# Two bottleneck blocks on one core: the 3x3 convolution with four products over the columns in every row combination, and its differences on VectorE

## The chip, the cores and the metric

The kernel runs on one core of one Trainium2 chip. Its time is the device time of one execution in microseconds (us): 1990.88 us, the median of 4 runs (1990.1 to 1991.1). One further execution was recorded by the hardware profiler; all durations below come from that one. TensorE is called PE in the profile, VectorE DVE, ScalarE ACT, GpSimd POOL and SyncE SP.

## The reference

Two residual blocks of the ResNet kind, one after the other, all in fp32, on 64 images of 1024 channels and 14x14 pixels:

```python
def block(x, w1, b1, g1, be1, w2, b2, g2, be2, w3, b3, g3, be3, residual_scale):
    out = relu(bn(conv1x1(x, w1, b1), g1, be1))          # 1024 -> 256 channels
    out = relu(bn(conv3x3(out, w2, b2, pad=1), g2, be2)) # 256 -> 256
    out = bn(conv1x1(out, w3, b3), g3, be3)              # 256 -> 1024
    return relu(x + softplus(residual_scale) * out)
```

`bn` normalises by the mean and variance over all images and pixels of that same batch, so each convolution has to be complete before the next may use its result.

## The kernel before

The inputs of a block are laid out with the channels on the 128 partitions. The intermediate result with 256 channels stays on the chip (`y_all`: 128 partitions, 2 channel slots, all pixels). The program has these stages: the first 1x1 convolution of block 0 (from the start to about 308 us), the 3x3 convolution of block 0 (`conv2`, about 309 to 601 us), statistics, then the last 1x1 convolution of block 0 fused with the first of block 1 (to about 1290 us), the 3x3 convolution of block 1 (about 1294 to 1587 us), statistics, and the last 1x1 convolution with the way out. Beside the first stage `filters` makes the transformed 3x3 filters on VectorE and ScalarE and stores them in HBM through GpSimd's DMA queue, in 11 steps (`FSTEPS`) for each of 8 pieces.

**How the 3x3 convolution is computed.** It is a fast algorithm in both directions. The images are in 8 groups of 8 (`NG`, `GI`). Along the rows, four output rows are made from six *row combinations* of input rows (`NF` = 6, numbered 0 to 5): sums and differences with small factors. Each combination is multiplied with its own transformed filter, and the six products are combined into four output rows. Per group they come in the order 1, 2, 3, 4, 5, 0, so that there are 48 items in all. A combination has 2 slots of 32 lines (24 for combinations 3 and 4) of 14 columns per partition, which is 896 (672) numbers per partition. The columns are stored as the 7 odd ones and then the 7 even ones.

**Over the columns**, `FOUR` says which combinations use the cheaper form: all but combination 1. There the product has four parts instead of five, each with 4 matrix products over 7 columns (2 input slots x 2 output slots; each matrix product appears as two MATMUL records, so 8 records):
- `m`, on the sum of the odd and the even half (`sums`, line 596, VectorE). ScalarE copies it into the two output banks `even` and `odd` (line 699).
- `l`, on the difference of the halves (`diffs`, line 599, GpSimd). ScalarE copies it to a tile `ls` (line 699, called from `later`).
- `even` and `odd`, added into those banks, on `v` (line 603, VectorE): differences of neighbouring columns; ScalarE fills the two border columns (lines 607 and 608).

VectorE then adds or subtracts `ls` when it takes the result out of the banks (`add`, line 752).

Combination 1 has no `diffs`, no `v` and no `l`: `even` and `odd` read the combination itself with two filters each, which is 16 records for each of the two instead of 8, and its result is taken straight from the banks into the two tiles `a` and `d` (lines 785 and 786, four instructions). Its `m` copy adds the convolution's bias (line 697).

**The order of the work.** `combine` makes the row combinations of a pair on VectorE (line 581 is the helper `stt`, for scalar_tensor_tensor; lines 641, 643 and 648 are further instructions) and `ready` makes `sums`, `diffs` and `v` and issues the loads of the filters. The loop at the end of `conv2` holds a queue of three items that are ready. For item k it issues, in this order: `middle` (`l`), the `even` part, `start` of item k+1 (`m` and the two copies), a long piece of work on ScalarE (`long_work`: the normalisation of the next group or a moment of the last), the `odd` part, and then `finished.send`, which takes the item out and combines results (`finish`, lines 766 to 839). After that it makes item k+3. A scheduler that runs when the program is built merges the streams of instructions; the matrix products and the lines with `keep_in_program_order` keep their order. Each engine then works its list strictly in order.

For the last of the four output rows' parts (item 0 of a group), `finish` writes `out_rows[0]` from the banks (line 833) and adds `a` by an accumulating DMA from GpSimd (line 838), except in the last group, where VectorE adds it (line 831). The moments of group g-1 that long_work takes on ScalarE during group g need these rows.

The buffers are counted in `BUFS`. At the very end, `residual` for the last images writes the output in four transfers of two channel slots each, issued by SP (line 1086).

Of the kernel before, what the change touches and what calls it, by code (L numbers as in the profile page):

```python
# [41 lines left out]
P = 128  # L42
# [3 lines left out]
CS = C // P  # L46
# [23 lines left out]
BUFS = dict(ua=3, ub=3, t=2, r=4, sums=3, diffs=4, v=3, ls=3, f=2, fa=2)  # L70
# [3 lines left out]
FOUR = 0, 2, 3, 4, 5  # L74
NKS = [4 if i in FOUR else 5 for i in range(NF)]
NK = max(NKS)

FSTEPS = 11
D1D2, D0, D3, D1, D2 = range(5)
# [12 lines left out]
def bottlenecks(ctx: ExitStack, tc: tile.TileContext, x, w1s, w2s, w3s, pars, out):  # L92
# [10 lines left out]
        [dram.tile([P, MS, MS, NKS[i], P], FP, tag=f"u{b}_{i}", name=f"u{b}_{i}") for i in range(NF)]  # L103
# [70 lines left out]
    def filters(pieces, spare):  # L174
# [11 lines left out]
        c1 = view(second, 18, 5)  # L186
# [18 lines left out]
        for piece, following in itertools.zip_longest(pieces, pieces[1:]):  # L205
# [6 lines left out]
            def out(i, u, a=0):  # L212
                nc.gpsimd.dma_start(out=us[b][i][:, s, o, a : a + u.shape[1]], in_=u)
# [18 lines left out]
            yield  # L232
            sums(c2, c2, r1, ALU.subtract)
            scaled(r2, 1.0 / 2)
# [9 lines left out]
            yield  # L244

            sums(g[:, 0], g[:, 0], g[:, 2], ALU.add)
            scaled(c4, 1.0 / 48)
            out(4, c4)
            yield
            sums(c1[:, :3], g[:, 0], g[:, 1], ALU.add)  # L250
            yield
            sums(c1[:, 3:], c1[:, 0:3:2], c1[:, 1:2].to_broadcast([P, 2, P]), ALU.subtract)
            scaled(c1, -1.0 / 6)
            for to, a, e in ((D0, 0, 1), (D1D2, 1, 2), (D3, 2, 5)):
                out(1, c1[:, a:e], to)
# [293 lines left out]
    def conv2(psum, pool, b, par, aff, affine_of, stats):  # L549
# [32 lines left out]

        def combine(g, pair, before=None):
# [4 lines left out]
            def ready(i, r):  # L588
                lines = (full if i in (3, 4) else RT) * GI
                r = r.rearrange("p s r (i w) -> p s (r i) w", i=GI)  # L590

                def half(tag):
                    return pool.tile([P, MS, RT * GI, WH], FP, tag=tag, name=tag, bufs=BUFS[tag])[:, :, :lines]

                sums, diffs = half("sums"), None
                nc.vector.tensor_add(sums, r[:, :, :, WH:], r[:, :, :, :WH])  # L596
                if i in FOUR:
                    diffs = half("diffs")
                    nc.gpsimd.tensor_sub(diffs, r[:, :, :, :WH], r[:, :, :, WH:])  # L599
                    v = pool.tile([P, MS * RT * GI * W], FP, tag="v", name="v", bufs=BUFS["v"])  # L600
                    v = v[:, : MS * lines * W].rearrange("p (s l c) -> p s l c", s=MS, c=W)
                    q = r.rearrange("p s l (q c) -> p (s l) q c", q=2)
                    nc.vector.tensor_sub(
                        v[:, :, :, 1 : W - 1].rearrange("p s l (q c) -> p (s l) q c", q=2),
                        q[:, :, :, 1:], q[:, :, :, : WH - 1],
                    )
                    nc.scalar.activation(v[:, :, :, 0], r[:, :, :, 0], AF.Copy)
                    nc.scalar.activation(v[:, :, :, W - 1], r[:, :, :, W - 1], AF.Copy, scale=-1.0)
                    r = v

                first = g == 0 and i == order[0][0]
                u = {}
                for tag, a, e in (("ub", 1, NKS[i]), ("ua", 0, 1)) if first else (("ua", 0, 1), ("ub", 1, NKS[i])):
                    n = MS * MS * (NK - 1 if a else 1) * P
                    v = pool.tile([P, n], FP, tag=tag, name=tag, bufs=BUFS[tag])
                    v = v[:, : MS * MS * (e - a) * P].rearrange("p (s o k m) -> p s o k m", s=MS, o=MS, m=P)
                    for part in [slice(1, 2), slice(0, 1)] if first else [slice(0, MS)]:
                        nc.sync.dma_start(
                            out=v[:, part].rearrange("p s o k m -> p (s o) (k m)"),
                            in_=us[b][i][:, part, :, a:e].rearrange("p s o k m -> p (s o) (k m)"),  # L620
                        )
                    u[a] = v
                return Products(i, lines, r, sums, diffs, u, first)

            def run(ins):
                if before is not None:
                    tc.keep_in_program_order(ins)

            both = slice(0, MS)
            if pair[0] == 1:  # L630
                t1, t2 = new("t"), new("t")
# [10 lines left out]
                yield ready(1, ra)  # L642
                nc.vector.tensor_sub(rb, t1, t2)  # L643
                yield ready(2, rb)
            elif pair[0] == 3:
                t3, t4 = (new("t", full) for i in range(2))
# [8 lines left out]
            else:  # L655
                last(ra, g, 2, -4.0)
                last(rb, g, 1, -1.0)
                for s in range(MS):
                    stt(rb[:, s, :full], rows(g, s, 3, 0, full), -5.0, rows(g, s, 5, 0, full))
                    stt(ra[:, s, :full], rows(g, s, 2, 0, full), -5.0, rows(g, s, 4, 0, full))  # L660
                for s in range(MS):
                    stt(rb[:, s, :full], rows(g, s, 1, 0, full), 4.0, rb[:, s, :full])
                yield ready(NF - 1, rb)
                for s in range(MS):
                    stt(ra[:, s, 1:], rows(g, s, 0, 1, RT), 4.0, ra[:, s, 1:])
                yield ready(0, ra)

        class Products:


            def __init__(self, i, lines, r, sums, diffs, u, first):
                self.i, self.lines, self.n = i, lines, lines * WH
                self.r, self.sums, self.diffs, self.u, self.first = r, sums, diffs, u, first
                self.four = i in FOUR
# [17 lines left out]
            def biased(self, to, m):  # L692

                for v in to:
                    if self.i == 1:
                        for o in range(MS):
                            nc.scalar.activation(v[:, o], m[:, o], AF.Identity, bias=par[:, B2 + o : B2 + o + 1])
                    else:
                        nc.scalar.activation(v, m, AF.Copy)  # L699

            def later(self, k, v, op):

                l = self.whole("l", k, v)
                ls = pool.tile([P, MS * RT * GI * WH], FP, tag="ls", name="ls", bufs=BUFS["ls"])
                self.ls, self.op = ls[:, : MS * self.n].rearrange("p (o n) -> p o n", o=MS), op
                self.biased([self.ls], l)

            def start(self):
# [3 lines left out]
                if not self.first:  # L712
                    self.biased(self.banks.values(), self.whole("m", 0, self.sums))

            def middle(self):
                if self.four:
                    self.later(DIFF, self.diffs, ALU.subtract)

            def columns(self, *qs):

                r = self.r
                if self.four:
                    parts = {ODD: [(0, WH, D3M1, r[:, :, :, WH:])], EVEN: [(0, WH, D0M2, r[:, :, :, :WH])]}
                else:
                    parts = {
                        ODD: [(0, WH, D1, r[:, :, :, WH:]), (0, WH - 1, D3, r[:, :, :, WH + 1 :])],
                        EVEN: [(0, WH, D2, r[:, :, :, :WH]), (1, WH, D0, r[:, :, :, : WH - 1])],
                    }
                steps = [(q, o, part, s) for q in qs for o in range(MS) for part in parts[q] for s in range(MS)]
                if self.first:  # L730


                    steps.sort(key=lambda step: -step[3])
                opened = set()
                for q, o, (a, e, k, v), s in steps:
                    to = self.banks[q][:, o].rearrange("p (l c) -> p l c", c=WH)[:, :, a:e]
                    matmul(
                        to, self.filter(s, o, k), v[:, s], start=self.first and q not in opened, stop=True,
                        skip_group_check=True,
                    )  # L740
                    opened.add(q)
                if self.first:
                    self.later(0, self.sums, ALU.add)
# [6 lines left out]
            def add(self, q, to, v):  # L750

                nc.vector.tensor_tensor(to, v, self.column(q, self.ls), ALU.add if q == EVEN else self.op)  # L752
# [11 lines left out]
        def finish():  # L764


            for g in range(NG):
                out_rows = [y_grp[:, :, g, k::4, :] for k in range(4)]
                last_group = g == NG - 1

                def stat(k, lines):
# [5 lines left out]
                fa = None if ca.ls is None else outputs(ca)  # L777
                fb = outputs((yield))
                a, d = new("fa"), new("fb")
                if fa is not None:  # L780
                    nc.vector.tensor_add(a, fa, fb)
                    nc.vector.tensor_sub(d, fa, fb)
                else:
                    for q in ca.banks:
                        nc.vector.tensor_tensor(half(a, q), ca.column(q), half(fb, q), ALU.add)
                        nc.vector.tensor_tensor(half(d, q), ca.column(q), half(fb, q), ALU.subtract)
# [31 lines left out]
                if last_group:  # L818
# [3 lines left out]
                for j, q in enumerate(cb.banks):  # L822
                    for o in range(MS):
# [6 lines left out]
                        if last_group:  # L830
                            nc.vector.tensor_add(to, bank, more)
                        else:
                            nc.vector.tensor_tensor(to, bank, ls, ALU.add if q == EVEN else cb.op)
                    stat(2 + j, [out_rows[0][:, o].rearrange("p r (i q c) -> p q r i c", i=GI, q=2)[:, q] for o in range(MS)])
                if not last_group:
# [54 lines left out]
        def long_work(g, k):  # L890
# [4 lines left out]
            if g + 1 == NG:  # L895
                i = (None, 0, 1, 2, 3, None)[k]
# [13 lines left out]
        for k in range(NG * NF):  # L910
            item, more = queue[0], queue[1:2]
            item.middle()
# [4 lines left out]
            elif more and more[0].four:  # L917
# [156 lines left out]
    def residual(psum, xt, b, t, w3, aff, made=()):  # L1074
# [3 lines left out]
        step = 2 if b == 1 and t == T - 1 else CS  # L1078
        for o in range(CS):
# [3 lines left out]
            nc.scalar.activation(v, v, AF.Relu, bias=shift[:, o : o + 1])  # L1083
            if (o + 1) % step == 0:
                queue = nc.gpsimd if step == CS else nc.sync
# [298 lines left out]
```

## Time and profile before

| | |
|---|---|
| median of 4 runs | 1990.88 us |
| the profiled execution, its own time | 1990.68 us |
| its span (first to last instruction) | 1988.9 us |
| around the span | 1.8 us |
| granted PE clock, mean of the span | 0.992 |
| DVE busy over the span | 1573.4 us (79%) |
| ACT busy | 956.0 us (48%) |
| POOL busy | 690.8 us (35%) |
| `conv2` of block 0 by the DVE timeline: first normalisation (line 545) at 309.24, first aggregation of the result (line 1168) at 601.16 | 291.9 us |
| `conv2` of block 1, the same two instructions at 1294.37 and 1586.34 | 292.0 us |

A row of the timeline gives the start, the duration, the engine, the line, the operation, the tiles (out<-in), the shape and how many instructions were merged in it. [...] In a row of groups, the numbers behind the bar are the busy time of the group, the mean duration in ns, and the time that the engine stood idle before them, with what ended it.

### The profile page before, as it was taken

The numbers are of one execution on the slowest core, as the hardware profiler recorded it, in microseconds if no ns is written. First come the engines' busy times: TensorE is split into PE (matmuls) and PEld (weight loads), VectorE is DVE, ScalarE is ACT, GpSimd is POOL, SyncE is SP. The second block draws the span as 40 slices with busy tenths as digits, with TensorE's granted clock in tenths as the row PEclk, the third lists the DMA queues.
The fourth block names the chain that finished last, engine by engine and source line by source line (L and its number), as shares of the span: only waits on it lengthen the run. The fifth ranks groups of instructions, "written<-read, shape, count | busy, mean of one in ns | idle before, by whom it ended". The sixth has DMA issues, their size and how long they took to land.

```text
span 1988.9 us, 27740 instructions
## 1 busy us (share of the span) xinstructions
PE 1941.7 (98%) x9560; PEld 1636.6 (82%) x9560; DVE 1573.4 (79%) x2844; ACT 956.0 (48%) x1947; POOL 690.8 (35%) x738
## 2 busy tenths in 40 slices
PE   8999999999998999999999999999999899999998
PEld 5555557899997889999999999989999887555554
DVE  5788758999888566776776777699999875899997
ACT  1222214556565055555555555445656541555555
POOL 0111101333325134334334334214242250666665
PEclk9999999999999999999999999999999999999999
DMA  7866725676757534444444444266777575699998
GB/s 272 290 248 249 260 98 173 176 206 203 204 163 201 193 130 162 168 190 162 172 185 162 177 181 163 98 206 179 210 201 205 145 194 206 247 338 333 342 337 296
DMA packets 191341, 414.09 MB, mean 208 GB/s; under 512 B 27296, under 2 KB 159040, under 8 KB 174688
## 3 DMA queue, kind: packets, MB, share of 16 engines
q1 hardware_dynamic: 161728, 329.06, 48.7%
q0 software_dynamic: 24000, 32.39, 7.1%
q10 hardware_dynamic: 5472, 50.86, 6.1%
q8 instruction: 76, 1.25, 0.3%
q14 instruction: 65, 0.53, 0.1%
HBM read 267.95 MB, written 115.87 MB: 193 GB/s over the span
## 4 chain that ended last, share of the span: by engine, by line
PE 81%; DVE 12%; DMA 3%; ACT 2%; issue 1%; SPq 1%; POOL 0%; DVEq 0%; ACTq 0%
PE ay L172 17%; PE cy L172 13%; PE cp L172 11%; PE ap L172 10%; PE even L172 6%; PE odd L172 6%; PE ax L172 5%; PE m L172 5%; PE cx L172 4%; PE l L172 4%; DMA x<-mid 2%; DVE x L456 2%; PE ps L172 1%; DVE sums L596 1%; DVE f L752 1%
## 5 line engine op out<-in xcount | busy, mean ns | idle before, releaser
L330 ACT ACTIVATE cu<-cy,scale 128x196 f32<-128x196 f32 (+1 forms) x552 | 257.1, 475 | 295.5 <-PE cy L172 287.8
L599 POOL TENSOR_TENSOR diffs<-r 128x448 f32<-128x448 f32 (+1 forms) x80 | 139.1, 1756 | 328.5 <-DVE r L643 155.4
L330 ACT ACTIVATE x<-x,shift 128x392 f32<-128x392 f32 x368 | 212.0, 614 | 69.1 <-POOL x L482 52.6
L456 DVE SCALAR_TENSOR_TENSOR x<-cp,scale,x 128x196 f32<-128x196 f32 (+1 forms) x368 | 177.9, 484 | 82.1 <-PE cp L172 81.0
L477 POOL TENSOR_TENSOR x<-x,cu 128x196 f32<-128x196 f32 (+1 forms) x184 | 167.4, 910 | 170.7 <-ACT cu L330 170.6
L172 PE MATMUL cy<-ct,ws 128*128 128x196 f32 (+1 forms) x736 | 221.7, 383 | 2.5 <-ACT cu L330 2.5
L172 PE MATMUL ay<-at,ws 128*128 128x196 f32 (+1 forms) x752 | 209.3, 381 | 1.0 <-ACT au L330 1.0
L482 POOL TENSOR_TENSOR x<-x,cu 128x392 f32<-128x392 f32 x124 | 125.9, 1015 | 190.8 <-DVE x L456 186.0
L172 PEld LDWEIGHTS ay<-at,ws 128*128 128x128 f32 x752 | 136.3, 190 | 35.1 <-ACT au L330 1.9
L172 PEld LDWEIGHTS cy<-ct,ws 128*128 128x128 f32 x736 | 133.6, 190 | 36.9 <-ACT cu L330 3.8
L503 POOL TENSOR_TENSOR x<-x,cu 128x392 f32<-128x392 f32 x120 | 125.1, 1043 | 82.6 <-DVE x L456 75.0
L172 PE MATMUL m<-sums,ua 128*128 128x224 f32 (+1 forms) x752 | 145.5, 336 | 0.0
L172 PEld LDWEIGHTS m<-sums,ua 128*128 128x128 f32 x752 | 131.3, 189 | 0.3
L456 DVE SCALAR_TENSOR_TENSOR x<-cx,scale,x 128x196 f32<-128x196 f32 (+1 forms) x184 | 89.1, 484 | 49.8 <-PE cx L172 49.6
L172 PE MATMUL even<-v,ub 128*128 128x224 f32 (+1 forms) x640 | 124.0, 335 | 2.7 <-ACT even L699 2.7
L172 PE MATMUL cy<-y,w 128*128 128x196 f32 (+1 forms) x404 | 126.5, 399 | 0.0
L172 PE MATMUL cx<-y,w 128*128 128x196 f32 (+1 forms) x404 | 125.3, 396 | 0.0
L172 PE MATMUL odd<-v,ub 128*128 128x224 f32 (+1 forms) x640 | 123.8, 335 | 0.2
L172 PE MATMUL l<-diffs,ub 128*128 128x224 f32 (+1 forms) x640 | 122.0, 333 | 0.0
L330 ACT ACTIVATE au<-ay 128x196 f32<-128x196 f32 (+1 forms) x141 | 53.7, 381 | 140.3 <-PE ay L172 139.6
L172 PE MATMUL cp<-zt 128*128 128x257 f32 x392 | 119.1, 385 | 1.7 <-DVE zt L987 1.7
L172 PE MATMUL cp<-y,ws 128*128 128x196 f32 (+1 forms) x368 | 113.8, 391 | 2.2 <-DVE x L456 0.5
(217 smaller groups left out, 4389.4 us busy)
## 6 DMA issues: line engine op xcount, KB each, us to landing
x<-in_x SPq DMA_DIRECT2D x62, 1568.0 KB, 6.8
ub<-u SPq DMA_DIRECT2D x80, 768.0 KB, 4.9
x<-mid SPq DMA_DIRECT2D x32, 1568.0 KB, 10.0
mid<-x ACTq DMA_DIRECT2D x31, 1568.0 KB, 5.1
out<-x SPq DMA_DIRECT2D x124, 392.0 KB, 6.6
ua<-u SPq DMA_DIRECT2D x94, 256.0 KB, 3.1
ub<-u SPq DMA_DIRECT2D x14, 1024.0 KB, 6.2
u<-y POOLq DMA_DIRECT2D x40, 256.0 KB, 6.1
```

The costliest lines, as they stand in the source:

```text
L172: tc.keep_in_program_order(nc.tensor.matmul(*args, **kw))
L330: tc.keep_in_program_order(nc.scalar.activation(*args, **kw))
L456: nc.vector.scalar_tensor_tensor(v, bank, self.scale[:, o : o + 1], v, ALU.mult, ALU.add)
L477: nc.gpsimd.tensor_add(self.part(1, 1), self.part(1, 1), u3)
L482: nc.gpsimd.tensor_add(v, v, self.u12)
L503: nc.gpsimd.tensor_add(v, v, self.u12[:, i * self.n : (i + 1) * self.n])
L596: nc.vector.tensor_add(sums, r[:, :, :, WH:], r[:, :, :, :WH])
L599: nc.gpsimd.tensor_sub(diffs, r[:, :, :, :WH], r[:, :, :, WH:])
L752: nc.vector.tensor_tensor(to, v, self.column(q, self.ls), ALU.add if q == EVEN else self.op)
```

## The change

- Combination 1 gets the four-part form too. It now has `diffs`, `v` and `l`; the `FOUR` distinction goes, and its result is taken out like the others (`outputs`), after which `a` and `d` are made by two instructions on 896 numbers. In the first item of all, where no bank holds `m` yet, PE adds the `m` product into both banks itself (8 records more than one `m` takes), and the bias is added by VectorE on the way out.
- `diffs` of all combinations move from GpSimd to VectorE.
- Combinations 5 and 0 are made from the differences t3, t4 that combinations 3 and 4 use: four instructions on 672 numbers instead of eight on 336. For that the tag `t` gets 4 buffers. ScalarE makes one more border row.
- In the first group, `sums`, `v` and `diffs` of combination 1 are made slot by slot, in program order, between the two slots' normalisations.
- The next-to-last group too adds `a` on VectorE instead of by the accumulating DMA (`by_transfer`), and the moments in the last group are issued one item earlier.
- `filters` makes four column filters for combination 1 instead of five (9 steps, one store instead of three per piece).
- The last output transfers are 2, 2, 2, 1 and 1 slots; the very last is issued by ScalarE.

The diff, cut to its core:

```diff
-BUFS = dict(ua=3, ub=3, t=2, r=4, sums=3, diffs=4, v=3, ls=3, f=2, fa=2)
+BUFS = dict(ua=3, ub=3, t=4, r=4, sums=3, diffs=4, v=3, ls=3, f=2, fa=2)
-FSTEPS = 11
+FSTEPS = 9
...
             sums(c2, c2, r1, ALU.subtract)
+            scaled(c1, -1.0 / 12)
+            out(1, c1)
...
-            sums(g[:, 0], g[:, 0], g[:, 2], ALU.add)
-            sums(c1[:, :3], g[:, 0], g[:, 1], ALU.add)
-            sums(c1[:, 3:], c1[:, 0:3:2], c1[:, 1:2].to_broadcast([P, 2, P]), ALU.subtract)
-            scaled(c1, -1.0 / 6)
-            for to, a, e in ((D0, 0, 1), (D1D2, 1, 2), (D3, 2, 5)):
-                out(1, c1[:, a:e], to)
...
-                if i in FOUR:
-                    diffs = half("diffs")
-                    nc.gpsimd.tensor_sub(diffs, r[:, :, :, :WH], r[:, :, :, WH:])
...
+                def make(self, part):
+                    r, v = self.r[:, part], self.v[:, part]
+                    run(nc.vector.tensor_add(self.sums[:, part], r[:, :, :, WH:], r[:, :, :, :WH]))
                     q = r.rearrange("p s l (q c) -> p (s l) q c", q=2)
+                    run(
+                        nc.vector.tensor_sub(
+                            v[:, :, :, 1 : W - 1].rearrange("p s l (q c) -> p (s l) q c", q=2),
+                            q[:, :, :, 1:], q[:, :, :, : WH - 1],
+                        )
                     )
+                    run(nc.vector.tensor_sub(self.diffs[:, part], r[:, :, :, :WH], r[:, :, :, WH:]))
...
                     run(nc.vector.tensor_add(ra[:, part], t1[:, part], t2[:, part]))
-                yield ready(1, ra)
+                    xa.make(part)
+                yield products(xa)
...
-                for s in range(MS):
-                    stt(rb[:, s, :full], rows(g, s, 3, 0, full), -5.0, rows(g, s, 5, 0, full))
-                    stt(ra[:, s, :full], rows(g, s, 2, 0, full), -5.0, rows(g, s, 4, 0, full))
-                for s in range(MS):
-                    stt(rb[:, s, :full], rows(g, s, 1, 0, full), 4.0, rb[:, s, :full])
+                r5, r0 = (r[:, :, :full] for r in (rb, ra))
+                nc.vector.tensor_sub(r5, rows(g, both, 5, 0, full), rows(g, both, 3, 0, full))
+                stt(r5, t4, -4.0, r5)
                 yield ready(NF - 1, rb)
-                for s in range(MS):
-                    stt(ra[:, s, 1:], rows(g, s, 0, 1, RT), 4.0, ra[:, s, 1:])
+                nc.scalar.activation(ra[:, :, 0, :], rows(g, both, 2, 0, 1)[:, :, 0, :], AF.Copy, scale=-1.0)
+                nc.vector.tensor_sub(ra[:, :, 1:], rows(g, both, 0, 1, RT), rows(g, both, 2, 1, RT))
+                stt(r0, r0, 4.0, t3)
+                nc.scalar.activation(ra[:, :, RT - 1, :], ra[:, :, RT - 1, :], AF.Copy, scale=4.0)
...
-                fa = None if ca.ls is None else outputs(ca)
+                fa = outputs(ca)
                 fb = outputs((yield))
                 a, d = new("fa"), new("fb")
-                if fa is not None:
-                    nc.vector.tensor_add(a, fa, fb)
-                    nc.vector.tensor_sub(d, fa, fb)
-                else:
-                    for q in ca.banks:
-                        nc.vector.tensor_tensor(half(a, q), ca.column(q), half(fb, q), ALU.add)
-                        nc.vector.tensor_tensor(half(d, q), ca.column(q), half(fb, q), ALU.subtract)
+                nc.vector.tensor_add(a, fa, fb)
+                nc.vector.tensor_sub(d, fa, fb)
...
+                by_transfer = g < NG - 2
...
-                i = (None, 0, 1, 2, 3, None)[k]
+                i = (0, 1, 2, 3, None, None)[k]
...
-        step = 2 if b == 1 and t == T - 1 else CS
+            step = CS if not tail else 1 if o + 2 >= CS else 2
...
-                queue = nc.gpsimd if step == CS else nc.sync
+                queue = nc.gpsimd if step == CS else nc.scalar if o + 1 == CS else nc.sync
```

## The prediction

> **What bounds the kernel now.** I read the page first, then the busy time by stretches, then the timelines of PE and DVE inside the 3x3 convolution, which is all that the change touches but the last microseconds.
>
> ```profile
> PE 1941.7 (98%) x9560; PEld 1636.6 (82%) x9560; DVE 1573.4 (79%) x2844; ACT 956.0 (48%) x1947; POOL 690.8 (35%) x738
> L599 POOL TENSOR_TENSOR diffs<-r 128x448 f32<-128x448 f32 (+1 forms) x80 | 139.1, 1756 | 328.5 <-DVE r L643 155.4
> ```
>
> By the page PE is the bound and DVE has a fifth to spare. That is an average. The stretches of block 0's `conv2` (us; then busy us and instructions of PE, PEld, DVE, ACT, POOL; clock; DMA share; GB/s) say otherwise:
>
> ```profile
> 309.20:353.30 44.10, 40.30 (x222) 38.12 (x220) 43.12 (x76) 18.95 (x45) 9.38 (x8) 1.00 0.68 215
> 353.30:427.00 73.70, 71.27 (x404) 69.44 (x405) 70.76 (x120) 42.28 (x90) 22.81 (x15) 1.00 0.67 191
> 427.00:565.20 138.20, 138.20 (x799) 137.31 (x798) 127.81 (x221) 83.66 (x173) 46.22 (x29) 1.00 0.71 204
> 565.20:601.20 36.00, 33.20 (x193) 32.63 (x191) 28.02 (x59) 20.23 (x41) 10.58 (x20) 1.00 0.42 115
> sum 292.00, PE 282.96 PEld 277.50 DVE 269.72 ACT 165.13 POOL 88.99; mean PE 70.74 PEld 69.38 DVE 67.43 ACT 41.28 POOL 22.25
> ```
>
> DVE is busy for 269.7 of the 292.0 us, flat out for the first 44, and 92% in the middle, where PE has no gap at all. Both engines are near the bound, so what counts is how many microseconds each gets back or is given. Its idle 22.3 us are two things: waits for results, 19.3 us in all, most of them of this kind (us in total, times, longest),
>
> ```profile
> DVE f L752 <- PE even L172: 10.9, 6, 2.3
> DVE f L752 <- PE odd L172: 4.6, 8, 2.1
> ```
>
> and some 3 us of short gaps, where an instruction needs the result of the one just before it.
>
> PE's timeline prices its side:
>
> ```profile
> 461.08 3.02 PE L172 MATMUL even<-r,ub 128*128 128x224 f32 x16
> 463.94 1.68 PE L172 MATMUL m<-sums,ua 128*128 128x224 f32 x8
> 465.45 3.02 PE L172 MATMUL odd<-r,ub 128*128 128x224 f32 x16
> 468.31 1.67 PE L172 MATMUL l<-diffs,ub 128*128 128x224 f32 x8
> 469.82 1.70 PE L172 MATMUL even<-v,ub 128*128 128x224 f32 x8
> ```
>
> Start to start, a part of 8 records takes 1.51 to 1.53 us, and one of combination 1's parts of 16 takes 2.86. The same `even<-r` row begins again at 495.75, so a group takes 34.67 us.
>
> DVE's timeline prices the other side:
>
> ```profile
> 478.90 1.09 DVE L641 TENSOR_TENSOR r<-t 128x896 f32<-128x896 f32 x1
> 479.91 0.50 DVE L752 TENSOR_TENSOR f<-odd,ls 128x336 f32<-128x336 f32 x1
> 480.33 0.95 DVE L603 TENSOR_TENSOR v<-r 128x768 f32<-128x768 f32 x1
> 481.19 0.62 DVE L596 TENSOR_TENSOR sums<-r 128x448 f32<-128x448 f32 x1
> 481.73 0.50 DVE L752 TENSOR_TENSOR f<-even,ls 128x336 f32<-128x336 f32 x1
> 482.14 1.08 DVE L643 TENSOR_TENSOR r<-t 128x896 f32<-128x896 f32 x1
> 483.33 0.63 DVE L596 TENSOR_TENSOR sums<-r 128x448 f32<-128x448 f32 x1
> 483.87 1.83 DVE L648 TENSOR_TENSOR t<-y 128x672 f32<-128x672 f32 x1
> ...
> 486.91 0.85 DVE L791 TENSOR_TENSOR fc<-f 128x672 f32<-128x672 f32 x1
> 487.68 0.84 DVE L648 TENSOR_TENSOR t<-y 128x672 f32<-128x672 f32 x1
> ```
>
> Each instruction starts about 0.08 us before the recorded end of the last one. So the prices, start to start, are: 336 numbers 0.42 us, 448 0.535, 672 0.77, 768 0.87, 896 1.01; elsewhere 576 takes 0.67 and 224 takes 0.30. Two more things stand here. From 482.14 to 483.33 is 1.19 instead of 1.01: `sums` needs the `r` just made, a gap of 0.18. And line 648 took 1.83 us at 483.87 but 0.84 at 487.68: GpSimd worked on `diffs` from 483.39 for 1.59 us. Taking every one of DVE's 471 instructions between 309.2 and 601.15 over the shortest of its form gives 17.2 us of such stretching; 15.2 of it lies within 0.3 us of a `diffs` of GpSimd.
>
> **The change, part by part** (one block; there are two).
>
> PE: combination 1 takes 1.51 + 2 x 2.86 = 7.23 us, after the change four parts of 1.52 = 6.07. That is 1.16 less in seven groups (the first item has 40 records either way, and cannot start its slots earlier): PE needs 33.5 us a group, 8.1 us less in a block. If PE alone set the time, both blocks would gain 16.
>
> DVE is given, at the prices above:
> - combination 1: `v` 0.87 and `diffs` 0.535; combination 2: `diffs` 0.535; 1.94 x 8 groups, and 0.2 for the halves of the first: 15.7
> - combinations 3 and 4: two `diffs` of 336, 0.84 x 8: 6.7
> - combinations 5 and 0: eight instructions of 336 (3.36) become four of 672 (3.08), and two `diffs` of 448 (1.07) come: 0.79 x 8: 6.3
> - taking combination 1 out: six instructions of 448 (3.21) become four of 448 and two of 896 (4.16): 0.95 x 7, and 0.13 in the first group, where four of 224 with the bias replace two of 448: 6.8
> - the next-to-last group's two additions of 448: 1.1
>
> Together 36.6 us. What it gets back is the stretching, since GpSimd has no `diffs` any more: between 15.2 and 17.2, I take 16. So DVE's busy time in the stage goes from 269.7 to 269.7 + 36.6 - 16 = 290.3, call it 290, against 292 that the stage takes now. **DVE becomes the bound**; a group costs it 34.5 us without a gap (the sum of the prices of its 58 instructions) where PE needs 33.5.
>
> The stage's length is then 290 and what DVE can't fill. Short gaps: 3 us now; the three new `diffs` and `v` per group hang on fresh results, but there is other work to put between; I take 4 (0 to 7). Waits: 19.3 now. They are there because PE is late; with PE a microsecond a group faster and DVE a group's 34.5 us deep in its own list, nearly all go. The bounds are 0 and 19.3; I take 2, near the lower end, because the stretch to 353.30, where DVE is loaded as it will be everywhere, has none. 290 + 4 + 2 = 296, 4 more than now.
>
> At nothing I cost: the shorter `filters` (in the stretch from 40 to 300 us PE is busy for all 260, DVE for 200; without that cover its sixteen fewer instructions on DVE would be worth some 6 us, at 0.3 to 0.5 each); ScalarE's added copies and border columns (about 1.2 us a group on an engine busy for 84 of 138 us; behind a late copy wait the banks and so PE, which will have a microsecond to spare); the accumulating DMA that goes from group 6; the four `t` buffers; the first item's loads on SP's queue, where `ua` (128 KB a slot, landing in 4.7 us) now goes ahead of `ub`, while PE's first matmul waits for DVE; the earlier moments, which free ScalarE about 1.6 us sooner at the stage's end, where DVE will be what is late. The start, where slot 0's normalisation now stands behind 1.07 us of slot 1's work, is already in DVE's sum.
>
> The end: the last transfer is 1 slot instead of 2, 196 KB less at the 296 GB/s of the last slice: 0.66 us; the issue from ScalarE may cost or save 0.3. I take -0.6.
>
> Sum: 2 x 4 - 0.6 = +7.4. The profiled execution took 1990.68 (span 1988.9 and 1.8 around it), 0.2 under the median of 1990.88; 1990.9 + 7.4 = **1998.3**.
>
> [...]
>
> **Rivals.**
> - *DVE packs without a gap (not slower).* Busy 269.7 + 36.6 - 17.2 = 289, no gaps, no waits: 3 less in a block, -6 - 0.6, **1984**. For it: DVE had no wait at all in its first 44 us, and nothing forces one while items are made three ahead. Against: the three dependent pairs a group that the scheduler leaves open today. It decides as soon as gaps and waits stay under 1.2 us a block.
> - *The waits stay.* DVE's list is fixed when the program is built; where it puts `f<-even` early, DVE still stops for PE, and a microsecond lost by the bounding engine is lost for good. All 19.3 kept: 290 + 4 + 19 = 313, +42 in all, **2033**; half kept, 2013. For it: 2.3 us before the same instruction in each steady group. Against: PE gets faster just there.
> - *The stretching is not GpSimd's.* Then the 16 stay: +32 more, **2030**. For it: 2 of the 17.2 us lie beside no `diffs`. Against: 1.83 and 0.84 for the same instruction, with and without one.
>
> **How the numbers follow.** Mine 0.50 (1989 to 2008: gaps 3 to 7, waits 0 to 4), the gapless 0.25, waits that stay 0.17, stretching 0.08. A measurement tells about 0.2% from no change, 1986.9 to 1994.9. Faster: the gapless case, 0.25. Same: the lower part of mine, 0.22. Slower: the rest, 0.53. The range leaves out the upper half of the second rival and the third: 1984 to 2016.
>
> **What would show it.** Right: DVE busy for 287 to 292 us in each stage; line 596 and 648 back at their short times everywhere; groups 34.6 to 35.6 us apart; PE with about a microsecond idle a group, ended by DVE. Wrong: DVE idle by 10 us or more with waits on `even`; stretched instructions without GpSimd; or groups under 34.5 us, which would mean a price above is too high.

## The result, and the profile after

The changed kernel takes **1988.41 us** (median of 39 runs, 1987.07 to 1989.92), the kernel before 1991.09 on the same chips (59 runs, 1989.43 to 1993.56). The ratio is 0.9987, 95% interval 0.9982 to 0.9991: 2.7 us (0.13%) less. That is clear of the noise, but smaller than the 0.2% from which the prediction counts a change, and it points the other way than the forecast of 1998.3. The profiled execution took 1989.38 us (before: 1990.68), its span is 1987.6 us (before: 1988.9).

The first line is the page's busy time by engine, the rest the busy time by stretches of block 0's 3x3 convolution, in the columns of the prediction:

```profile
PE 1927.4 (97%) x9432; PEld 1620.3 (82%) x9432; DVE 1603.3 (81%) x2890; ACT 976.1 (49%) x2007; POOL 540.6 (27%) x638
```

```profile
309.10:353.20 44.10, 37.91 (x208) 35.73 (x207) 43.14 (x86) 19.00 (x46) 0.14 (x2) 1.00 0.61 197
353.20:427.00 73.80, 71.67 (x407) 70.57 (x406) 73.63 (x125) 47.54 (x101) 5.19 (x4) 1.00 0.69 191
427.00:565.00 138.00, 133.75 (x764) 131.64 (x763) 137.65 (x230) 88.71 (x184) 10.27 (x8) 1.00 0.70 195
565.00:598.80 33.80, 30.64 (x177) 30.09 (x175) 33.63 (x65) 20.37 (x47) 2.59 (x14) 1.00 0.34 110
sum 289.70, PE 273.98 PEld 268.03 DVE 288.05 ACT 175.63 POOL 18.19; mean PE 68.49 PEld 67.01 DVE 72.01 ACT 43.91 POOL 4.55
```

The page alone still makes PE the bound. In the stage it is the other way round: DVE is idle for 1.65 of 289.7 us, and PE now has gaps in the middle, where before it had none. PE's timeline shows where:

```profile
453.13 1.69 PE L169 MATMUL even<-v,ub 128*128 128x224 f32 x8
455.88 1.75 PE L169 MATMUL m<-sums,ua 128*128 128x224 f32 x8 [1.06 <-issue]
...
487.95 1.69 PE L169 MATMUL even<-v,ub 128*128 128x224 f32 x8
490.70 1.56 PE L169 MATMUL m<-sums,ua 128*128 128x224 f32 x7 [1.06 <-issue]
```

One gap of 1.06 us a group, 34.82 us apart (490.70 - 455.88), ahead of combination 1's `m`. The page ascribes it to nothing ("issue"), but DVE's timeline has the cause: the `sums` that this `m` reads is recorded to 455.78.

```profile
453.63 1.08 DVE L648 TENSOR_TENSOR r<-t 128x896 f32<-128x896 f32 x1
454.63 0.62 DVE L753 TENSOR_TENSOR f<-odd,ls 128x448 f32<-128x448 f32 x1
455.17 0.61 DVE L603 TENSOR_TENSOR sums<-r 128x448 f32<-128x448 f32 x1
455.70 0.95 DVE L606 TENSOR_TENSOR v<-r 128x768 f32<-128x768 f32 x1
456.57 0.62 DVE L611 TENSOR_TENSOR diffs<-r 128x448 f32<-128x448 f32 x1
457.10 0.85 DVE L808 TENSOR_TENSOR y<-fb,f 128x672 f32<-128x672 f32 x1
```

Every row starts before the recorded end of the last and is at its short price. Between `r` and the `sums` that needs it stands an `f` of another item: the short gap the prediction charged for is filled with other work.

Taking every DVE instruction of the stage at the short, undisturbed start-to-start time of its operation and shape in these traces ("work"), the rest of the stage can be split into stretched instructions, gaps behind the instruction just before (including the lost overlap of 0.08), and waits for other engines. The split depends on what is taken as undisturbed: with the very shortest single times 5 to 7 us of each column move from work to the rest, and the differences between columns change by up to 2.5 us. In us, block 0, with the experiments that matter most:

| | before | after | before, differences on DVE | after, five parts in combination 1 | five parts in groups 0, 1, 3, 5 |
|---|---|---|---|---|---|
| stage, block 0 | 291.92 | 289.69 | 288.48 | 286.64 | 282.06 |
| stage, block 1 | 291.97 | 292.77 | 288.52 | 286.70 | 282.12 |
| DVE's work | 246.8 | 283.3 | 266.2 | 265.0 | 274.1 |
| stretched | 20.7 | 2.5 | 4.6 | 4.4 | 2.8 |
| gaps | 4.9 | 3.9 | 4.8 | 3.1 | 3.2 |
| waits | 19.5 | 0 | 12.9 | 14.1 | 2.0 |

So 36.5 us of work went in, and 18.2 of stretching, 1.0 of gaps and 19.5 of waits came out. Block 1 is 3.1 us longer than block 0, with the same instructions. The same rows of both blocks' first item on PE, block 0 first:

```profile
319.12 1.02 PE L169 MATMUL even<-sums,ua 128*128 128x224 f32 x4 [3.22 <-DVE sums L603]
319.98 0.92 PE L169 MATMUL odd<-sums,ua 128*128 128x224 f32 x4
...
1301.32 1.86 PE L169 MATMUL even<-sums,ua 128*128 128x224 f32 x4 [3.10 <-DVE sums L603]
1302.97 1.70 PE L169 MATMUL odd<-sums,ua 128*128 128x224 f32 x4
```

After a gap of 3.10 us in block 1 four records take 1.70 instead of 0.92, and the granted clock says why:

```profile
1300.00:1305.00 5.00, 3.68 (x10) 3.35 (x11) 5.00 (x9) 0.92 (x4) 0.00 (x0) 0.57 0.29 100
1305.00:1310.00 5.00, 5.00 (x22) 4.73 (x21) 3.86 (x7) 0.79 (x4) 0.00 (x0) 0.75 0.18 52
```

The sixteen records from 1301.32 take 6.14 us where a full clock gives about 3.04 (four times 0.76, the step from 314.20 to 314.96 on PE in block 0, at a clock of 1.00). The clock was at 0.50 from 1300.7 to 1307.5 us. Before, this gap was 1.21 us, and the eight records behind it took 1.69 us at a clock of 1.00. Whether the clock falls behind this gap differs from run to run (e3 below lost some in both blocks: 0.94 and 0.83 over ten microseconds), so a part of the changed kernel's time is chance.

Outside the stages: up to the first 309.14 (before 309.24), between them 692.46 (693.21), and 400.09 (398.92) behind the second up to the last computation. The last transfer took 3.44 us behind ScalarE's last instruction, 3.64 before. In the stretch from 75 to 100 us behind block 1's stage the clock was 0.80, and 0.86 before. An experiment with the changed kernel's code there (e8) had 0.86 and 399.38 us, so a part of this is chance. Not all of it need be: this last stretch takes 399.19 to 401.47 us in the eleven profiled runs with the changed code and 398.87 and 398.92 in the two with the old. No run separates a cause.

### The profile page after: what moved, and what is told of

Same layout as the page of the kernel before. It is cut to its first block, busy times and chain, and to the rows that moved or that the text cites. A ratio compares the mean times of both kernels' runs of the same rounds, so it can differ in the third digit from the quotient of the medians.

```text
span 1987.6 us, 27403 instructions
## 1 busy us (share of the span) xinstructions
PE 1927.4 (97%) x9432; PEld 1620.3 (82%) x9432; DVE 1603.3 (81%) x2890; ACT 976.1 (49%) x2007; POOL 540.6 (27%) x638
## 4 chain that ended last, share of the span: by engine, by line
PE 88%; DVE 6%; DMA 2%; issue 1%; ACT 1%; SPq 0%; POOL 0%; DVEq 0%; ACTq 0%
PE ay L169 17%; PE cy L169 14%; PE cp L169 11%; PE ap L169 10%; PE even L169 7%; PE m L169 7%; PE odd L169 7%; PE l L169 7%; PE ax L169 5%; PE cx L169 4%; DVE x L447 2%; DMA x<-mid 1%; PE ps L169 1%; DVE x L505 1%; DVE ct L412 0%
## 5 line engine op out<-in xcount | busy, mean ns | idle before, releaser
L169 PE MATMUL odd<-v,ub 128*128 128x224 f32 (+1 forms) x768 | 151.7, 338 | 0.0
L169 PE MATMUL even<-v,ub 128*128 128x224 f32 (+1 forms) x768 | 151.5, 338 | 0.0
L169 PE MATMUL l<-diffs,ub 128*128 128x224 f32 (+1 forms) x768 | 148.8, 337 | 0.0
L169 PEld LDWEIGHTS m<-sums,ua 128*128 128x128 f32 x752 | 130.5, 189 | 20.7 <-issue 20.4
L836 POOL DMA_DIRECT2D y<-fa x24 | 31.1, 1530 | 414.4 <-ACT ls L719 225.6
L169 PEld LDWEIGHTS odd<-v,ub 128*128 128x128 f32 x768 | 135.4, 189 | 1.4
L169 PEld LDWEIGHTS even<-v,ub 128*128 128x128 f32 x768 | 135.3, 189 | 1.4
L169 PEld LDWEIGHTS l<-diffs,ub 128*128 128x128 f32 x768 | 134.8, 189 | 0.5
```

The source lines that it names most:

```text
L169: tc.keep_in_program_order(nc.tensor.matmul(*args, **kw))
L836: nc.gpsimd.dma_start(out=out_rows[0][:, o], in_=a[:, o], accum_op=ALU.add)
```

## The experiments

Theory: DVE bounds the changed stage, and the moved differences pay because GpSimd's were stretching DVE. Rivals: PE or a wait is the bound; the stretching has another cause; the gain comes from the cheaper row combinations.

### Which engine is the bound: more PE, more DVE

e3 repeats half of combination 1's `l` in 14 groups (0.75 us of PE each), e4 its `sums` (0.535 us of DVE each); both results are made twice and used once.

```diff
+                if self.i == 1 and not self.first:          # e3, in middle
+                    for s in range(MS):
+                        matmul(
+                            l[:, 0], self.filter(s, 0, DIFF), self.diffs[:, s].rearrange("p l c -> p (l c)"),
+                            start=(s == 0), stop=(s == MS - 1),
+                        )
...
+                    if self.i == 1 and before is None:      # e4, in make
+                        nc.vector.tensor_add(self.sums[:, part], r[:, :, :, WH:], r[:, :, :, :WH])
```

> The changed kernel; PE computes one half of the l product of combination 1 twice, 4 records or 0.75 us more in 14 of the 16 groups. The result is the same. Theory (VectorE bounds, PE idles by about a microsecond a group): the time moves by 0 to +3 us against the changed kernel, 1988 to 1991.5. Rival (PE still bounds): +10.5 us, 1999.

> The changed kernel; VectorE makes the sums of combination 1 twice, one instruction on 448 numbers or 0.535 us more in 14 of the 16 groups. The result is the same. Theory (VectorE bounds): +7.5 us against the changed kernel, 1994 to 1998. Rival (PE bounds, VectorE has slack): 0 to +2, 1988 to 1990.5.

Measured: e3 1988.32 us (ratio to before 0.9984, 0.9975 to 0.9993), groups 34.81 us, PE without its gap. e4 1998.02 (1.0032, 1.002 to 1.0043), groups 35.29, 0.47 more. PE has room for three quarters of a microsecond a group and DVE has none: DVE is the bound. The groups show it better than the times, because the clock comes in between. e3's stages are 291.43 and 291.38 us, each 1.7 over block 0 of the changed kernel, since the clock fell behind the gap of the first item in both of its blocks (the clock is the third number from the end):

```profile
310.00:320.00 10.00, 5.37 (x24) 4.70 (x24) 9.33 (x25) 3.25 (x10) 0.14 (x2) 0.94 0.81 270
1300.00:1310.00 10.00, 7.95 (x34) 7.63 (x35) 9.90 (x17) 2.43 (x10) 0.00 (x0) 0.83 0.32 104
```

At 0.50 a mean of 0.83 over ten microseconds is 3.4 us, and 3.4 us at half speed are the 1.7 us by which each stage is longer; the changed kernel had none of it in block 0 and 6.83 us in block 1. e4's clock, in the mean of the span, was 0.990 in three of its six executions (1996.67 to 1997.14 us) and 0.988 in the other three (1998.89 to 1999.91); that adds to its 9.6 us over the changed kernel, where the theory had 7.5.

### The differences alone, and everything but the differences

e2 is the kernel before with its 40 `diffs` a block on VectorE or, seen the other way, the change's first part alone. e1 is the changed kernel with its `diffs` on GpSimd.

```diff
-                    nc.gpsimd.tensor_sub(diffs, r[:, :, :, :WH], r[:, :, :, WH:])       # e2, from before
+                    nc.vector.tensor_sub(diffs, r[:, :, :, :WH], r[:, :, :, WH:])
...
-                    run(nc.vector.tensor_sub(self.diffs[:, part], r[:, :, :, :WH], r[:, :, :, WH:]))   # e1, from after
+                    nc.gpsimd.tensor_sub(self.diffs[:, part], r[:, :, :, :WH], r[:, :, :, WH:])
```

> The kernel before, with only its 40 differences of a stage moved to VectorE; combination 1 keeps its five-part product. Theory: 19.5 us of work come and 18.1 us of stretching go, VectorE stays at about 271 us busy in 292, groups stay 34.67 us apart as PE still bounds; total 1988 to 1992 us, line 648 and 596 back at their short times. Rival (stretching not GpSimd's): VectorE at 289 of 292 us busy with stretched instructions, total 2000 us or more.

> The changed kernel, with the 48 differences of a stage moved back to GpSimd. Theory (VectorE is the bound of the 3x3 stage, and GpSimd's differences stretch VectorE's instructions by about as much as the same differences cost on VectorE itself): 23.6 us of work leave VectorE per stage and 40 differences stretched it by 18.1 us before, so 48 bring 21.7 back; VectorE busy about 286 us per stage against 288.2, total 1984 to 1990 us. Rival (the stretching is not GpSimd's, so that the differences are simply 47 us of work given to VectorE): PE becomes the bound with 33.5 us a group, total 1970 to 1978 us.

Measured: e2 **1984.73** (0.9964, 0.9951 to 0.9976), below what was expected; e1 **1999.95** (1.004, 1.0027 to 1.0052), above it. e2's first two group intervals are 36.64 and 34.67 us (before: 38.27 and 36.50), all later ones 34.67 as before. What is left of the waits in its block 0:

```profile
DVE f L752 <- PE even L172: 4.9, 5, 1.0
DVE f L752 <- PE odd L172: 4.3, 7, 2.1
```

DVE has 19.4 us more work here and 16.1 less stretching, and is busy for 3.4 us more (273.2 against 269.8), yet the block is 3.4 us shorter. All of that lies in the first two intervals (1.63 and 1.83 us): DVE was the bound only there (in the first 80 us of the stage 8.2 us of stretching went, and eleven differences, 5.4 us, came). Behind it stands PE with its 34.67. In e1 DVE is stretched by 33.3 us in block 0, 0.7 for each `diffs` of GpSimd (48 and one for the halves of the first). GpSimd's timeline (its own row first), then DVE's:

```profile
473.53 1.63 POOL L611 TENSOR_TENSOR diffs<-r 128x448 f32<-128x448 f32 x1 [1.31 <-DVE r L572]
```

```profile
474.05 1.59 DVE L603 TENSOR_TENSOR sums<-r 128x448 f32<-128x448 f32 x1
475.56 0.61 DVE L753 TENSOR_TENSOR f<-odd,ls 128x448 f32<-128x448 f32 x1
```

The `sums` beside GpSimd's instruction takes 1.59 us, the same one alone 0.61.

Counting the DVE instructions of block 0 that are over 0.15 us longer than is usual for their operation and shape, there are 20 before (15.2 us together) and 48 in e1 (31.1 us), all beside a `diffs` of GpSimd, and none in any run with the differences on DVE. The rival that the stretching isn't GpSimd's falls. All of these instructions have both sources in SBUF; none of those that started beside a `diffs` and read the banks of a product, in PSUM, (107 in the two traces) is longer by more than 0.02 us. And 67 of the 68 end after GpSimd's instruction by their own usual duration less 0.1 us (here 475.64 - 475.16 = 0.48, against 0.61), as if they had waited for its end.

### Combination 1 in five parts, and the shared rows undone

e5 keeps the change but for combination 1's product, which has its five parts back, and with it the five column filters (11 steps) and, in the first group, one `sums` behind both slots instead of the slot-by-slot start. e10 also makes combinations 5 and 0 by the old eight instructions.

```diff
+FIVE = (0, 1, 2, 3, 4, 5, 6, 7)      # e5: groups whose combination 1 has five parts
...
+                    self.four = i != 1 or g not in FIVE
...
+                    if not self.four:
+                        self.v = self.r
+                        return
...
-                nc.vector.tensor_sub(r5, rows(g, both, 5, 0, full), rows(g, both, 3, 0, full))     # e10 as well
-                stt(r5, t4, -4.0, r5)
+                for s in range(MS):
+                    stt(rb[:, s, :full], rows(g, s, 3, 0, full), -5.0, rows(g, s, 5, 0, full))
...
```

> The changed kernel with combination 1 put back to its five-part product in all groups; everything else of the change stays (differences on VectorE, shared differences, last transfers, moments). Its fifth filter comes by a load of its own into a v buffer. Theory (the four-part product of combination 1 is the part that costs: it moves a stage that PE bounds at 34.67 us a group to one that VectorE bounds at 34.82, and opens the 3 us gap of PE at the start): like the kernel before with the differences on VectorE, groups of 34.67, and the shared differences take 0.3 us off each of the first two groups: 1982 to 1985.5 us. Rival (the four-part product gains and something else of the change takes it): slower than the changed kernel, 1990 or more.

> The kernel with five parts everywhere (1979.45), but the row combinations 5 and 0 are made by the old eight instructions without shared differences. Theory: from the third group on PE is the bound in that kernel (34.67 us per group, VectorE waits 14.1 us per stage), so the cheaper rows count only in the two groups at the start that VectorE bounds: 0.5 to 2.5 us more, 1980 to 1982. Rival: the shared differences are what separates that kernel from the kernel before with its differences on VectorE (1984.73): 1983.5 or more.

Measured: e5 **1979.45** (0.9945, 0.9931 to 0.9959), below what was expected, group intervals 35.69 and then 34.67; e10 1981.44 (0.9952, 0.994 to 0.9965), 36.64 and then 34.67. The times alone can't tell these two apart, the profiles can: the first interval differs by 0.95 us, all others are equal. The shared rows count only where DVE bounds, at the start. By stages, block 0: differences on VectorE -3.4 (e2), the rest of the change without the shared rows -0.9 (e10), the shared rows -1.0 (e5), **the four-part product in combination 1 +3.1** (after). In block 1 that last step costs 6.1, half of it the clock. The part that takes 1.16 us a group from PE makes the kernel slower, since it gives DVE more than it could take. Most of that arises in the first group: e7 below, with five parts there alone, has stages of 287.01 and 287.43 us, 2.7 and 5.3 under the changed kernel's and only 0.4 and 0.7 over e5's. These runs don't separate the product in that group from its slot-by-slot start.

### The gap at the start of a block

e8 puts three products that nothing uses into PE's gap of the first item.

```diff
+                    if self.first and n == len(steps) // 2:
+                        spare = self.bank("m").rearrange("p o n -> p (o n)")
+                        for _ in range(3):
+                            matmul(spare, ident, ident[:, :1].to_broadcast([P, MS * self.n]), start=True, stop=True)
```

> The changed kernel; in the first item of each stage PE makes three matmuls of 448 columns with the identity into a bank that is overwritten later (2.3 us), where it idles for 3.1 us waiting for slot 0. The result is the same. Theory (that gap, coming after other short ones, makes the chip lower PE's clock in the second block: 0.57 and 0.75 in the stretches from 1300 to 1310 us, eight matmuls at half speed): the clock stays at 1.00 there, the second stage goes from 292.8 to 289.7 us as in the first block, total 1985 to 1986.5. Rival (the gap is not the cause): 1988 to 1990.

Measured: 1984.31 (0.997, 0.9958 to 0.9981), a little below what was expected. The stages are 289.64 and 289.68 us: block 1 is as long as block 0. The ten microseconds that had a clock of 0.57 and 0.75:

```profile
1300.00:1310.00 10.00, 10.00 (x56) 9.94 (x55) 9.97 (x20) 3.21 (x10) 0.00 (x0) 1.00 0.40 133
```

So the 3.1 us are the clock's, and come from the gap: with it filled, the clock of these ten microseconds is 1.00 instead of 0.66, and the stage takes 289.68 us instead of 292.77. How long a gap it takes was not shown: in the changed kernel the clock fell behind 3.10 us in block 1 and stayed at 1.00 behind 3.22 us in block 0, and in e3 it fell behind this item's gap in both blocks (0.94 and 0.83).

### Some groups with five parts

PE needs 33.5 us for a group with four parts and 34.67 with five; DVE takes 34.8 for the first kind (the intervals of 34.82) and some 2.3 less for the second (283.3 and 265.0 us of work in eight groups). A mixture should balance them. The intervals are counted from behind combination 1 of one group to behind that of the next, so the first of the seven holds combination 1 of group 1. The edit is e5's with other groups in `FIVE`: 0, 2, 4, 6 (e6), 0 alone (e7), 0, 1, 3, 5 (e9), 0, 1, 4 (e11).

> As the last one, but combination 1 has five parts in the groups 0, 2, 4 and 6 and four parts in 1, 3, 5 and 7 (filters are made for both). Theory (each engine has its own total, and items made three ahead level them out): PE needs 34.67 and 33.5 us in turn, 34.1 on average, VectorE 34.8 and some 32.4, 33.6 on average, so groups 34.1 apart on average and 0.55 x 14 = 8 us less than with five parts everywhere: 1975 to 1979 us. Rival (nothing is levelled; each group goes at the pace of its own bound): 34.67 and 34.82 in turn, 1983 to 1987 us.

> As the last one, but five parts in group 0 alone. Theory: groups 1 to 7 at 34.82 as in the changed kernel, VectorE has some 2.9 us less in the first group and PE's gap of 3.1 us there shrinks to the 1.3 of the kernel before, so that the slow matmuls at 1301 us do not come: 2 x 2.5 + 3 less than the changed kernel, 1979 to 1983 us. Rival (the start is hidden behind the rest): within 1 us of the changed kernel, 1987.5 to 1989.5.

Measured: e6 1976.58 (0.9926, 0.9914 to 0.9939), e7 1980.80 (0.9952, 0.9939 to 0.9964). e7's intervals are 33.52, 35.16 and then 34.82: DVE bounds again. e6's are 33.52, 39.50, then 33.52 and 34.67 by turns. The 39.50 is one gap of PE with slow products behind it (granted clock 0.66 from 383 to 388 us):

```profile
378.14 1.68 PE L172 MATMUL l<-diffs,ub 128*128 128x224 f32 x8
382.75 2.18 PE L172 MATMUL m<-sums,ua 128*128 128x224 f32 x8 [2.93 <-issue]
384.73 2.98 PE L172 MATMUL even<-v,ub 128*128 128x224 f32 x8
```

> As the changed kernel, but combination 1 takes the five-part product over the columns in groups 0, 1, 3 and 5, and the four-part product in groups 2, 4, 6 and 7. With five parts in every group the first two group intervals were 35.69 and then 34.67 us and the time 1979.45; with five parts in groups 0, 2, 4 and 6 the intervals alternated between 33.52 and 34.67 except for one of 39.5 us, behind a gap of PE of 2.93 us, and the time was 1976.58. Theory: the interval of 39.5 us came because the first two groups are bounded by VectorE, which had nothing in hand when a four-part group came second; with five parts in groups 0 and 1 the start is as with five parts everywhere, and the alternation follows without the stall, 1.5 to 3 us less per stage than in the kernel with 0, 2, 4 and 6: 1970 to 1973.5. Rival: the first four-part group stalls PE wherever it stands, so the stall only moves to group 2: 1975 to 1978.

> As the changed kernel, but with five parts for combination 1 in groups 0, 1 and 4 and four parts in groups 2, 3, 5, 6 and 7. Theory: three five-part groups are enough for VectorE to stay ahead, so that the groups take about 33.9 us on the mean: 1971 to 1976. Rival: VectorE can't be levelled over two or three four-part groups in a row (the buffers between it and PE hold less than a group's 1.3 us of surplus), so these take 34.8 us, no less than a five-part group: 1977 or more.

Measured: e9 **1970.15** (0.9896, 0.9881 to 0.9911), the fastest here and 1% under the kernel before; e11 1972.54 (0.9905, 0.9892 to 0.9919). Both theories held. e9's intervals are 35.69, 33.52, 34.67, 33.52, 34.67, 33.52, 33.52, and no gap is left behind the first group. The middle of its block 0, by stretches:

```profile
353.20:427.00 73.80, 73.80 (x425) 73.33 (x424) 73.44 (x125) 47.03 (x98) 7.74 (x6) 1.00 0.74 204
427.00:565.00 138.00, 138.00 (x793) 137.10 (x792) 137.49 (x235) 88.98 (x189) 7.68 (x6) 1.00 0.68 199
```

PE and DVE are both full. e11's stages are nearly as long (282.48 and 282.20), with three groups of four parts at 33.52 in a row: the items made ahead hold more than the rival granted. Of its 2.4 us over e9, 0.5 lie in the stages, 0.6 ahead of the first and 1.2 behind the second in the profiled executions.

## Why the prediction was wrong

**The step that failed** is "290 + 4 + 2 = 296, 4 more than now". In block 0 all three terms were too high, and together they turned what became a gain of 2.2 us into a loss of 4: measured were 288.1 us busy and 1.6 idle (288.4 and 4.4 in block 1), where it had 290 and 6. By stage the change is -2.2 and +0.8 us instead of +4 each. The mechanism, that DVE becomes the bound, was right.

- *Busy, 290.* It was 1.9 too high. The work added was right: 36.6 predicted, 36.5 in the table. The stretching that goes was taken as 16 ("between 15.2 and 17.2, I take 16") and is 18.2 in the table, of which the 15.2 us of strongly stretched instructions are sure: I had taken the shortest time by line and form, and some lines never ran undisturbed. Line 781 runs once a block, at 2.06 us before and 1.09 in e2. By operation and shape alone the stretching before is 20.7, not 17.2. The busy time stayed within "287 to 292".
- *Gaps, 4 (0 to 7).* This is the term furthest off, by 2.4 us in block 0. Alone it doesn't turn the sign (290 + 1.6 + 2 is still 1.7 over 291.9); with the other two it does. The new `diffs` and `v` do read fresh results, but the scheduler put another item's instruction between, so that DVE's idle time apart from waits fell from some 3 us to 1.6, of which 0.96 stand in the first 44 us (44.10 - 43.14) and 0.7 in all the rest.
- *Waits, 2.* None in block 0 and 2.6 in block 1. Taking them near zero was right as a consequence of PE's 33.5 us (measured 33.52 where PE bounds). "The waits stay" fell, but only for the changed kernel: with five parts in combination 1 14.1 us of them do stay.
- *The start, costed at nothing* because it "is already in DVE's sum". For DVE it is. For PE it makes the first item's gap 3.1 to 3.2 us instead of 1.2 to 1.3, and the clock that it loses in block 1 comes back as DVE's wait of 2.6. e8 takes 3.1 us out of that stage by filling the gap. That it was lost in block 1 and not in block 0 of this execution is luck: e3 lost some in both (0.94 and 0.83 over ten microseconds).
- *The end, -0.6* was -0.2. The page shows the transfer only as a few microseconds behind the last computation, and a slot less is not its whole price.
- *The rivals.* "DVE packs without a gap", 1984, is what block 0 did: -2.2, against -3 worked out. With block 1's clock the time fell between it and the likeliest case, whose own range, 1989 to 2008, it missed by 0.6; the range of 1984 to 2016 held it. "The stretching is not GpSimd's" fell (e1).

What was right: DVE becomes the bound; groups of 34.82 us in "34.6 to 35.6", PE with a microsecond idle a group. A price per group good to 0.3 us still left the sign open: it is the difference of 36.5 us put in and 38.7 taken out a block.

Not seen at all was that the parts have opposite signs. Moving the differences is worth 6 to 7 us by itself, the rest without combination 1 another 4 to 5, and combination 1 gives back about 9 (from the medians 1991.09, 1984.73, 1979.45 and 1988.41, or each against the kernel before of its own session), most of it in the first group (e7: 1980.80).

The prices held: in the changed kernel too the rows overlap by 0.08 us, and a `diffs` of 448 takes 0.53 us (456.57 to 457.10), where the prediction had 0.535.

A `diffs` of GpSimd stretches DVE by 0.45 us on average in the kernel before and by 0.7 in e1. The count above says why: about every second one met an instruction of DVE that it could stretch before (20 for 40), and nearly every one in e1 (48 for 49), by 0.76 and 0.65 us each. DVE has 1.5 us of idle time in that block of e1 instead of 22.2; that this is why more of them met is likely, but not shown apart from where the scheduler put them.

## What to carry to other kernels

When two engines are within a few per cent of each other, a part that unloads one by loading the other has to be dosed: choose for how many tiles it is used, so that both end together (here the four-part product in four groups of eight: 1970 us, against 1979 in none and 1988 in all). Price each part of a change in its own sum, with the engine that is the bound before and behind it; a total near zero hides a gain and a loss. Count a gap of PE at the start of a stage also as a risk to its clock: here it was at 0.50 for 6.83 us behind one of 3.10 us, at a price of 3.1 us.

## What the runs showed of the hardware

- GpSimd's `tensor_sub` of 128x448 or 128x336 costs VectorE 0.4 to 0.7 us on average, about as much as the 0.535 or 0.42 us that VectorE takes to do it itself. Moving it to GpSimd saved nothing where VectorE is the bound (e1: 1999.95 us against 1988.41). The cost fell on instructions of VectorE with both sources in SBUF (67 of 68 ended when GpSimd's was through and their own time over), and not on those that read PSUM (107, at most 0.02 us longer).
- PE's clock fell to 0.50 for 6.83 us (1300.7 to 1307.5) behind a gap of 3.10 us (changed kernel, block 1). It also fell behind the same item's gap in both blocks of e3 (0.94 and 0.83 over ten microseconds) and behind one of 2.93 us (e6: 0.66 from 383 to 388 us, eight records 2.98 us instead of 1.69). It stayed at 1.00 behind one of 3.22 us (changed kernel, block 0) and behind 1.34 and 1.21 us (the kernel before).
